# Two graph layers on one core: pauses in rows of gathers, row copies inside layer 1, a first copy on VectorE, x loads on SyncE

## The chip, the cores and the metric

The kernel runs on one core of a Trainium2 chip. The metric is the time of one execution on the device, in microseconds. Three runs of the kernel before took 2118.67, 2122.86 and 2124.68 us; the median, 2122.86 us, is the time that the change is compared with. A change of less than 0.3% of it, about 6.4 us, can hardly be told from no change.

## The reference

There are 4096 nodes with 512 features each, and a symmetric adjacency matrix `adj` of 4096 x 4096, of which some 0.8% is not zero. The two layers are, cut to what matters:

```python
# layer 0
h = relu(layernorm(x))
d = rowsum(adj) ** -0.5
x = x + relu((d[:, None] * adj * d[None, :]) @ h @ W0 + b0)
# layer 1
h = relu(layernorm(x))
e = leaky_relu(h @ W1 @ a_top + (h @ W1 @ a_bottom).T, 0.2)
p = softmax(where(adj > 0, e, -1e12))
n = -softmax(where(adj > 0, -e, -1e12))
x = x + elu(concat([p @ h, n @ h]) @ wtrans)
```

Layer 0 is a dense product with all of `adj`. In layer 1 only the places where `adj` is not zero count, so each row needs just the h rows of its neighbours.

## The kernel before, in words

**Layer 0.** The 4096 rows are 32 tiles of 128 rows, numbered j. The output tiles are made in eight groups, `GROUPS = ((26, 6), (16, 4), (20, 4), (0, 4), (4, 4), (8, 4), (12, 4), (24, 2))`, each given as its first tile and number of tiles. Group 0 is multiplied plainly while the rows of `adj` are summed and x is normalized and projected. The other groups multiply 2 x 2 blocks with seven products in place of eight (`multiply_blocks`, L893, on the sums that `sum_at` makes at L880 to L883). A group of four holds seven of the eight PSUM banks, so the next group's products can begin only as the banks of the last one are read out. `join_blocks` (L764 to L797) does that at the start of the next group: ScalarE copies half a bank (L773), VectorE adds another half to it (L774), and three to five more VectorE instructions follow for every pair of output tiles. Then `finish0` (from L803) makes the result of one tile at a time: it adds x (L806), stores x1 for later, normalizes, makes h, and writes h into the tables (L813 to L824).

**Tables.** Layer 1 gathers rows from eight tables in DRAM, one for each eighth of the output rows. All have the same h rows (516 words) and each has its own mask bytes (128 words). `tab0`, which is 4, is the table that layer 1 reads first. `finish0` writes h to `tab0` by a GpSimd DMA (L814), and to the other seven by `put_row` (L443): for most tiles seven ScalarE DMAs (L821 to L823); for the tiles 12 to 15, that is `GROUPS[-2]`, the 28 puts are collected in `puts` and issued by SyncE at the end of the last group (L1213 to L1214); for the tiles 24 and 25, the last group, SyncE writes table 0 (L819) and ScalarE writes the six others within layer 1, one for each of the first 12 row blocks (L1362 to L1364).

**x.** `load_xr` (L743 to L745) loads the x tile that `finish0` adds. It is a GpSimd DMA. There are two buffers, so the load for the third and fourth tile of a group waits until VectorE has used the first and second one.

**Lists.** VectorE makes, for every pair of row blocks, lists of the rows that it needs (L391, L393), and GpSimd scatters these (L413), one indirect DMA after the other.

**Layer 1.** There are 64 row blocks of 64 rows, in pairs. For a pair 22 chunks of 128 rows are gathered, in three parts a = 0, 1, 2 of 8, 6 and 8 chunks; each chunk is one indirect DMA on GpSimd (L451) of 128 rows of 2576 bytes. The even block of a pair uses the parts 0 and 1, the odd block 1 and 2. VectorE and ScalarE make the weights of a block (`scores` L463, `exps` L469 to L473, `mask_out` L480, `tree` L485 to L491), TensorE multiplies 14 chunks (L1305), ScalarE scales the result (L1314), TensorE turns it (L506) and, once a pair, multiplies by wtrans (L1328). The first pair, `PAIR0`, is gathered and begun within the last group of layer 0: `gather0(1)`, `gather0(2)` and `gather0(0)` are called at the steps 4, 7 and 10 of that group. A verdict on the lists (L1027 to L1030) is then loaded by every engine, which branches to `sparse_layer1`. Its first gathers are the three parts of `pairs[0]`, then of `pairs[1]`. In `gather1` a small GpSimd copy that reads the last chunk of part 2 (L1269 to L1273) keeps GpSimd from going on before that chunk has landed; it is there for the pairs with index k = 1 to 5.

**Order.** The framework's scheduler places instructions on each engine by its own estimate of when they are ready; `keep_in_program_order` ties one behind all that was written for its engine before it. An instruction that waits holds up all that is queued behind it on its engine, DMA issues on SyncE, ScalarE and GpSimd included.

Of the kernel before, what the change touches and what calls it, by code (L numbers as in the profile page):

```python
# [259 lines left out]
def gcn_gat_kernel(  # L260
# [181 lines left out]
    def put_row(queue, g, j, h):  # L442
        return queue.dma_start(  # L443
            out=rows_of(g, j // EJ)[:, j % EJ, :ROW_W], in_=h.bitcast(I32)
        )

    def gather(gt, n, a):

        c = sum(CHUNKS[:a])
        for k in range(CHUNKS[a]):  # L450
            nc.gpsimd.indirect_dma_start(  # L451
                out=gt[:, k, :],
                out_offset=None,
                in_=table[2 * n // RPT],
                in_offset=bass.IndirectOffsetOnAxis(
                    ap=idx[n // NH][:, n % NH, c + k : c + k + 1], axis=0
                ),
            )
# [56 lines left out]
    with sbuf(name="y0", bufs=1) as y_pool, sbuf(name="wa", bufs=1) as wa_pool, sbuf(name="bits", bufs=4) as bits_pool, sbuf(name="small0", bufs=4) as small, ExitStack() as rest, ExitStack() as lists:  # L515
# [226 lines left out]

        def load_xr(j):  # L743
            xrs[j] = xin.tile([P, F], F32, tag="xr", name=f"xr{j}")
            nc.gpsimd.dma_start(out=xrs[j], in_=x[j * P : (j + 1) * P, :])  # L745

        def affine(y, acc, j):

# [16 lines left out]
        def join_blocks(i0, n, acc, work, new_w):  # L765

            ys = {}
            for x in range(n // 2):
                p16, p23, p45, p7 = acc[x]
                j0, j1 = i0 + x, i0 + n // 2 + x  # L770
                ys[j0], ys[j1] = y, v = [new_y(work, j, -1) for j in (j0, j1)]
                w = new_w(f"w{j0}")[:, :H]
                nc.scalar.copy(y[:, :H], p16[:, :H])  # L773
                nc.vector.tensor_tensor(w, p16[:, H:], y[:, :H], ALU.add)  # L774
                nc.vector.tensor_tensor(y[:, H:], p45[:, H:], w, ALU.add)

                def first(p23=p23, y=y):
                    nc.vector.tensor_tensor(y, p23, y, ALU.add)

                def second(p7=p7, w=w, p45=p45, v=v):  # L780
                    two = "p (a f) -> p a f"
                    nc.vector.tensor_tensor(w, p7, w, ALU.add)
                    nc.vector.tensor_tensor(
                        v.rearrange(two, a=2),
                        p45.rearrange(two, a=2),
                        w.unsqueeze(1).to_broadcast([P, 2, H]),
                        ALU.add,
                    )

                if n == 2:  # L790
                    first()
                    affine(y, y, j0)
                    second()
                    affine(v, v, j1)
                else:
                    second()
                    first()  # L797
            if n > 2:
                for j, y in ys.items():
                    affine(y, y, j)  # L800
            return ys

        def finish0(work, j, y, h, prod):  # L803

            xt = xrs.pop(j)
            nc.vector.scalar_tensor_tensor(y, y, 0.0, xt, ALU.max, ALU.add)  # L806
            nc.gpsimd.dma_start(out=x1_dram[j], in_=y)
            nc.gpsimd.memset(h[:, ROW_T + 1 :], 0.0)
            normalize(h[:, :F], y, f"b{j}")

            def dot(g, vec):
                nc.vector.scalar_tensor_tensor(
                    prod(f"prod{j}_{g}"), h[:, :F], 1.0, wa_bc[g], ALU.mult, ALU.mult, accum_out=vec  # L813
                )  # L814

            dot(1, h[:, ROW_T : ROW_T + 1])
            put_row(nc.gpsimd, tab0, j, h)
            if late0 <= j < late0 + n_late:
                put_row(nc.sync, 0, j, h)  # L819
            elif GROUPS[-2][0] <= j < sum(GROUPS[-2]):  # L820
                puts.extend(partial(put_row, nc.sync, g, j, h) for g in others)  # L821
            else:
                for g in others:  # L823
                    put_row(nc.scalar, g, j, h)  # L824
            dot(0, s_all[:, j : j + 1])
            nc.vector.tensor_copy(t_all[:, j : j + 1], h[:, ROW_T : ROW_T + 1])
# [156 lines left out]
                mark()  # L983
        pending = (GROUPS[0], partial(evict, i0, acc))
        listing, joining, spare = [], [], []
        puts = []

        def make_lists(g):
            make_keys(g)
# [130 lines left out]
        with sbuf(name="work2", bufs=2) as work, sbuf(name="sums2", bufs=2) as sum_pool, sbuf(name="at2", bufs=4) as at_pool, sbuf(name="scratch", bufs=1) as scratch, sbuf(name="pair", bufs=1) as pair:  # L1120
# [7 lines left out]
            def gather0(a):  # L1128
                if a < 2:
                    k = 1 - a  # L1130
                    gt = y_pool.tile([P, Y_PARTS[k] * F], F32, tag=f"y{k}", name=f"g0_{a}")
                else:
                    gt = t_pool.tile([P, T_PARTS[0] * 3 * H], F32, tag="t0", name=f"g0_{a}")
                gt = gt[:, : CHUNKS[a] * ROW].bitcast(I32)
                gts[a] = gt.rearrange("p (k c) -> p k c", c=ROW)
                gather(gts[a], PAIR0, a)

            def parts0(r):
                a = r % 2
# [59 lines left out]
            def step(jp):  # L1199
                if jp == 0:  # L1200
                    nc.scalar.dma_start(
                        out=s_pair,
                        in_=s_dram[PAIR0 * P : (PAIR0 + 1) * P].partition_broadcast(P),
                    )
                if jp == 4:
                    gather0(1)
                if jp == 7:
                    gather0(2)
                if jp == 10:
                    gather0(0)  # L1210
                    weights0(blocks[0])
                if jp == NP - 1:
                    for put in puts:  # L1213
                        tc.keep_in_program_order(put())  # L1214
                    weights0(blocks[1])
                    warm = small.tile([P, 1], F32, tag="warm", name="warm2", bufs=1)
                    tc.keep_in_program_order(
                        nc.scalar.activation(warm, ones[:, 0:1], AF.Sqrt)
                    )
# [20 lines left out]
    def sparse_layer1():  # L1240
        with ExitStack() as pools:
# [22 lines left out]
            def gather1(n, a):  # L1264
                k = pairs.index(n)
                gt = g_pools[k % 2, a].tile([P, CHUNKS[a], ROW], I32, tag="g", name=f"g{a}_{n}")
                gather(gt, n, a)
                gath.setdefault(n, []).append(gt)
                if a == 2 and 0 < k < 6:  # L1269

                    mark = small.tile([P, 1], I32, tag="mark", name=f"mark{n}", bufs=1)
                    i = nc.gpsimd.tensor_copy(mark, gt[:, CHUNKS[a] - 1, 0:1])
                    tc.keep_in_program_order(i)  # L1273

            def parts(r):

# [67 lines left out]
            pairs = [(PAIR0 + n) % (NR // 2) for n in range(1, NR // 2)]  # L1344
            order = [r for n in pairs for r in (2 * n, 2 * n + 1)]
            first = order[:4]
            later = [*range(tab0 + 1, NTAB), *range(1, tab0)]
            wanted = list(dict.fromkeys(r // 8 for r in order))
            for _ in range(2):
                tc.keep_in_program_order(load_s(wanted.pop(0)))  # L1350
# [8 lines left out]
            weights(order[1])  # L1359
            for k, r in enumerate(order):  # L1360
                product(r)
                if k < n_late * len(later):  # L1362
                    g, m = later[k // n_late], k % n_late
                    tc.keep_in_program_order(put_row(nc.scalar, g, late0 + m, late_h[:, m]))  # L1364
                if k + 4 - k % 2 < len(order):
                    for a in ((0,), (1, 2))[k % 2]:
                        gather1(order[k + 4 - k % 2] // 2, a)
# [20 lines left out]
        sparse_layer1()  # L1388
    with branch.Else():
        dense_layer1(  # L1390
            tc, adj_t, wtrans, out, x1_dram, table[0], s_all, t_all, ident, ones, load_adj_t, bank
        )


# [28 lines left out]
```

## Time and profile before

| What | Value |
|---|---|
| Median of the timed runs | 2122.86 us |
| The profiled execution's own time | 2154.57 us |
| Its span | 2153.1 us |
| TensorE busy | 2010.9 us, 93% |
| VectorE busy | 1115.9 us, 52% |
| ScalarE busy | 517.8 us, 24% |
| GpSimd busy | 942.3 us, 44% |
| Mean DMA rate | 243 GB/s |
| Mean granted TensorE clock | 0.969 |

A line of the waits view reads: the engine and its line, what released it, total idle time in us, times, longest. A line of the windows view gives for a stretch of time each engine's busy time with its number of instructions, the granted TensorE clock, the mean busy share of the 16 DMA engines and GB/s. A line of the timeline gives start, duration, engine, line, operation, tiles, and in brackets the idle time before and its releaser. "issue" is idle time for which the profile shows no wait, "remote" a release of which it doesn't know the source. PE is TensorE's matmul, PEld its weight load, DVE is VectorE, ACT is ScalarE, POOL is GpSimd and SP is SyncE.

### The profile page before, as it was taken

The page shows a single profiled execution, that of the slowest core. Times are in us where ns is not written, and L with a number is a line of the kernel's source. Part 1 is how long each engine was busy: PE and PEld are TensorE (multiplying, and loading weights), DVE is VectorE, ACT ScalarE, POOL GpSimd, SP SyncE. Part 2 cuts the span into 40 slices and gives each one's busy share as a digit, 9 for nine tenths or more (in the row PEclk, how much of TensorE's full clock was granted, in tenths as well). Part 3 has the DMA queues.
Part 4 walks back from the last instruction along what each step waited for, and adds up shares of the span by engine and source line. Part 5 has one row for each costly group of instructions (what it writes and reads, how often), then busy time and mean ns, then how long its engine had stood idle before and what let it go on. Part 6 is the DMA issues. An engine that isn't in the chain of part 4 may idle for free.

```text
span 2153.1 us, 20102 instructions
## 1 busy us (share of the span) xinstructions
PE 2010.9 (93%) x6456; PEld 1184.8 (55%) x6456; DVE 1115.9 (52%) x2791; ACT 517.8 (24%) x889; POOL 942.3 (44%) x1017
## 2 busy tenths in 40 slices
PE   7998999999998979899639999999999999999998
PEld 3443447888776868787414444444444444444443
DVE  5444536463896469834605645445354455455441
ACT  4645612223331310001102221212122222122120
POOL 2010102121123310323365767777777777777740
PEclk9999999999998989999869999999999999999999
DMA  9988918796977885456787878878788888888850
GB/s 376 367 300 326 366 35 295 256 317 197 338 222 245 259 251 174 150 181 191 271 260 224 267 239 254 253 239 242 235 255 242 251 240 238 254 242 239 246 179 21
DMA packets 186441, 524.12 MB, mean 243 GB/s; under 512 B 25683, under 2 KB 34867, under 8 KB 186326
## 3 DMA queue, kind: packets, MB, share of 16 engines
q0 software_dynamic: 73856, 283.61, 43.2%
q1 hardware_dynamic: 82592, 184.90, 25.2%
q10 hardware_dynamic: 29878, 54.24, 7.1%
q8 instruction: 52, 0.85, 0.2%
q14 instruction: 63, 0.52, 0.1%
HBM read 419.73 MB, written 102.92 MB: 243 GB/s over the span
## 4 chain that ended last, share of the span: by engine, by line
PE 55%; DVE 5%; another core or an unknown queue 3%; issue 1%; ACT 0%; DMA 0%; DVEq 0%; ACTq 0%
PE u L1305 35%; PE o L1328 10%; PE p L893 8%; PE tp L506 1%; DVE keys L393 1%; DVE lst L391 1%; PE cs L496 0%; DVE p L480 0%; DVE sums L880 0%; DVE sums L881 0%; DVE sums L882 0%; DVE sums L883 0%; DMA at<-in_adj_t 0%; DVE y L749 0%
## 5 line engine op out<-in xcount | busy, mean ns | idle before, releaser
L451 POOL DMA_INDIRECT g<-table,idx x704 | 751.0, 1067 | 283.5 <-issue 196.5
L1305 PE MATMUL u<-g,p 128*128 128x512 f32 x1736 | 762.8, 596 | 3.4 <-DVE p L480 3.1
L1305 PEld LDWEIGHTS u<-g,p 128*128 128x128 f32 x1736 | 325.7, 191 | 392.0 <-issue 379.1
L893 PE MATMUL p<-y,at 128*128 128x256 f32 x832 | 255.2, 389 | 18.5 <-DVE w L774 7.1
L893 PE MATMUL p<-t,sums 128*128 128x256 f32 x832 | 251.7, 387 | 14.9 <-DVE sums L881 9.6
L463 DVE TENSOR_TENSOR z<-g,s 128x512 f32<-128x512 f32 (+1 forms) x124 | 77.3, 624 | 353.8 <-DMA g<-table,idx 285.3
L893 PE MATMUL p<-y,sums 128*128 128x256 f32 x832 | 253.4, 387 | 2.4 <-issue 2.4
L1328 PE MATMUL o<-wt_sb,ut 128*128 128x512 f32 x512 | 225.1, 592 | 0.5 <-ACT ut L510 0.5
L473 ACT ACTIVATE p<-z 128x896 f32<-128x896 f32 (+2 forms) x136 | 115.8, 900 | 307.1 <-issue 220.2
L893 PEld LDWEIGHTS p<-y,at 128*128 128x128 f32 x832 | 159.8, 194 | 45.6 <-DVE w L774 8.0
L893 PEld LDWEIGHTS p<-t,sums 128*128 128x128 f32 x832 | 159.9, 194 | 43.0 <-DVE sums L881 13.7
L852 PE MATMUL acc<-y,at 128*128 128x512 f32 x384 | 176.4, 597 | 2.4 <-ACT y L700 2.4
L893 PEld LDWEIGHTS p<-y,sums 128*128 128x128 f32 x832 | 161.8, 195 | 26.0 <-issue 2.8
L480 DVE SCALAR_TENSOR_TENSOR p<-g,p 128x384 f32<-128x384 uint8 (+1 forms) x256 | 143.3, 620 | 56.8 <-ACT p L473 34.2
L725 POOL DMA_DIRECT2D table<-m x71 | 54.2, 765 | 258.1 <-ACT m L714 127.7
L1328 PEld LDWEIGHTS o<-wt_sb,ut 128*128 128x128 f32 x512 | 94.8, 190 | 107.8 <-issue 107.1
L714 ACT ACTIVATE m<-at 128x1024 uint8<-128x1024 f32 (+1 forms) x110 | 105.6, 988 | 193.6 <-DMA at<-in_adj_t 146.8
L893 PE MATMUL p<-t,at 128*128 128x256 f32 x416 | 127.7, 389 | 18.5 <-DVE w L774 17.2
L677 PE MATMUL yp<-w_sb,hx_t 128*128 128x512 f32 x256 | 124.6, 633 | 15.8 <-ACT y L700 13.4
L1314 ACT ACTIVATE us<-u,rl 128x512 f32<-128x512 f32 x62 | 42.6, 687 | 354.2 <-issue 203.4
L880 DVE TENSOR_TENSOR sums<-at 128x256 f32<-128x256 f32 x104 | 43.3, 417 | 149.8 <-PE p L893 87.1
L852 PEld LDWEIGHTS acc<-y,at 128*128 128x128 f32 x384 | 71.2, 192 | 81.5 <-issue 78.4
(183 smaller groups left out, 1746.3 us busy)
## 6 DMA issues: line engine op xcount, KB each, us to landing
at<-in_adj_t SPq DMA_DIRECT2D x136, 512.0 KB
ar<-in_adj SPq DMA_DIRECT2D x128, 512.0 KB
table<-h ACTq DMA_DIRECT2D x182, 258.0 KB
table<-m POOLq DMA_DIRECT2D x55, 256.0 KB
at<-in_adj_t SPq DMA_DIRECT2D x32, 384.0 KB
g<-table,idx POOLq DMA_INDIRECT x704
xr<-in_x POOLq DMA_DIRECT2D x32, 256.0 KB
x<-x1d SPq DMA_DIRECT2D x32, 256.0 KB
```

The source lines that it names most:

```text
L451: nc.gpsimd.indirect_dma_start(out=gt[:, k, :], out_offset=None, in_=table[2 * n // RPT], in_offset=bass.IndirectOffsetOnAxis(ap=idx[n // ...
L463: return nc.vector.tensor_tensor(z, t.to_broadcast([P, n, RB]), s.unsqueeze(1).to_broadcast([P, n, RB]), ALU.add)
L473: nc.scalar.activation(p[:, :, g, :], z, AF.Exp, scale=(1.0, -1.0)[g])
L480: nc.vector.scalar_tensor_tensor(e, m, 0.0, e, ALU.is_gt, ALU.mult)
L677: nc.tensor.matmul(yp, hx_t[j][:, c * P : (c + 1) * P], w0_sb[:, c, :], start=c == 0, stop=c == FC - 1,)
L714: nc.scalar.activation(m, at, AF.Sign)
L725: nc.gpsimd.dma_start(out=rows_of(t, e)[:, c:, ROW_W + (a - t * TT) * P // 4 : ROW_W + (b - t * TT) * P // 4], in_=masks[i0][:, c:, (a - i ...
L852: nc.tensor.matmul(a, at[:, 0, it * P : (it + 1) * P], y0[j], start=j == 0, stop=j == NJ - 1)
L880: op(t[:, 0], a[:, :, 0, 1], a[:, :, 1, 1], ALU.add)
L893: i = nc.tensor.matmul(out, left[:, x * P : (x + 1) * P], right, start=jp == 0 and first, stop=jp == NP - 1 and (final or not first),)
L1305: nc.tensor.matmul(u, p[:, k0 + k].rearrange("p g c -> p (g c)"), gt[:, k, :F].bitcast(F32), start=k0 + k == 0, stop=k0 + k == nk - 1,)
L1328: nc.tensor.matmul(po, ut[:, g, c, :], wt_sb[:, g * FC + c, :], start=g == 0 and c == 0, stop=g == 1 and c == FC - 1,)
```

## The change

Four edits. A helper `pause` holds the small GpSimd copy, and it is called at three more places: after `gather0(2)` in the last group of layer 0, after part 1 of `pairs[0]` and after part 0 of `pairs[1]`. The h rows of the tiles 12 to 15 and 24 to 25 are no longer put into the other tables from SBUF; within layer 1, at the row blocks k = 1, 7, 13, 19, 25, 31 and 37, SyncE issues two DMAs that copy these 768 rows from `tab0` to one other table, from DRAM to DRAM. The first copy of `join_blocks` goes from ScalarE to VectorE, and `load_xr` from GpSimd's queue to SyncE's. The other branch, which doesn't run here, reads `tab0` in place of table 0.

```diff
+    def pause(pool, gt):
+        mark = pool.tile([P, 1], I32, tag="mark", name="mark", bufs=1)
+        i = nc.gpsimd.tensor_copy(mark, gt[:, gt.shape[1] - 1, 0:1])
+        tc.keep_in_program_order(i)
...
         def load_xr(j):
             xrs[j] = xin.tile([P, F], F32, tag="xr", name=f"xr{j}")
-            nc.gpsimd.dma_start(out=xrs[j], in_=x[j * P : (j + 1) * P, :])
+            nc.sync.dma_start(out=xrs[j], in_=x[j * P : (j + 1) * P, :])
...
-                nc.scalar.copy(y[:, :H], p16[:, :H])
+                nc.vector.tensor_copy(y[:, :H], p16[:, :H])
...
             put_row(nc.gpsimd, tab0, j, h)
-            if late0 <= j < late0 + n_late:
-                put_row(nc.sync, 0, j, h)
-            elif GROUPS[-2][0] <= j < sum(GROUPS[-2]):
-                puts.extend(partial(put_row, nc.sync, g, j, h) for g in others)
-            else:
+            if all(not j0 <= j < j0 + n for j0, n in GROUPS[-2:]):
                 for g in others:
                     put_row(nc.scalar, g, j, h)
...
                 gather(gts[a], PAIR0, a)
+                if a == 2:
+                    pause(small, gts[a])
...
                 if jp == NP - 1:
-                    for put in puts:
-                        tc.keep_in_program_order(put())
                     weights0(blocks[1])
...
-                if a == 2 and 0 < k < 6:
-                    mark = small.tile([P, 1], I32, tag="mark", name=f"mark{n}", bufs=1)
-                    i = nc.gpsimd.tensor_copy(mark, gt[:, CHUNKS[a] - 1, 0:1])
-                    tc.keep_in_program_order(i)
+                if (k, a) in ((0, 1), (1, 0)) or a == 2 and 0 < k < 6:
+                    pause(small, gt)
...
-            later = [*range(tab0 + 1, NTAB), *range(1, tab0)]
+            later = [*range(tab0 + 1, NTAB), *range(tab0)]
+            def copy_rows(g, j, n):
+                r = j // EJ * ER + j % EJ * P
+                return nc.sync.dma_start(
+                    out=table[g][r : r + n * P, :ROW_W], in_=table[tab0][r : r + n * P, :ROW_W]
+                )
...
-                if k < n_late * len(later):
-                    g, m = later[k // n_late], k % n_late
-                    tc.keep_in_program_order(put_row(nc.scalar, g, late0 + m, late_h[:, m]))
+                if k % 6 == 1 and k // 6 < len(later):
+                    for j, n in GROUPS[-2:]:
+                        tc.keep_in_program_order(copy_rows(later[k // 6], j, n))
```

More of the change, by code (lines that the diff above doesn't have):

```diff
@@ L985, in gcn_gat_kernel @@
         listing, joining, spare = [], [], []
-        puts = []
         def make_lists(g):
@@ L1390, in gcn_gat_kernel @@
         dense_layer1(
-            tc, adj_t, wtrans, out, x1_dram, table[0], s_all, t_all, ident, ones, load_adj_t, bank
+            tc, adj_t, wtrans, out, x1_dram, table[tab0], s_all, t_all, ident, ones, load_adj_t, bank
         )
```

## The prediction

> **What bounds the kernel now.** I read the page first, then the windows, the waits of TensorE, and the timeline where it stands still. TensorE is the bound nearly everywhere, so only its idle time is for sale.
>
> ```profile
> span 2153.1 us, 20102 instructions
> PE 2010.9 (93%) x6456; PEld 1184.8 (55%) x6456; DVE 1115.9 (52%) x2791; ACT 517.8 (24%) x889; POOL 942.3 (44%) x1017
> ```
>
> That leaves 142 us. Some 30 us of it lie in group 0, which the change doesn't touch. For the rest, the windows (the gathers in layer 0's last group; the start of the layer 1 gathers; the stretch after it; layer 1's steady part):
>
> ```profile
> 1008.00:1040.00 32.00, 21.45 (x92) 16.91 (x91) 6.46 (x15) 1.54 (x2) 21.15 (x22) 0.90 0.96 344
> 1070.35:1088.00 17.65, 17.65 (x39) 7.39 (x38) 2.28 (x9) 0.76 (x3) 13.46 (x14) 0.88 0.78 229
> 1088.00:1131.50 43.50, 5.46 (x19) 2.88 (x17) 0.65 (x4) 2.02 (x4) 28.46 (x30) 0.58 0.82 253
> 1300.00:2060.00 760.00, 759.70 (x1979) 350.85 (x1978) 373.39 (x692) 158.51 (x261) 562.06 (x519) 1.00 0.82 244
> ```
>
> The steady part has no idle TensorE: nothing is to be gained there, only lost. From 1088 to 1131.5 us TensorE, VectorE and ScalarE all do next to nothing while GpSimd issues gather upon gather. Who waits for whom there, on TensorE, and in layer 0 from 300 us on:
>
> ```profile
> PE tp L506 <- ACT us L1196: 25.3, 1, 25.3
> PE tp L506 <- issue: 12.8, 1, 12.8
> PE ok_ps L1027 <- DVE all_ok L1024: 7.3, 1, 7.3
> ...
> PE p L893 <- DVE w L774: 24.3, 5, 7.8
> PE p L893 <- issue: 10.4, 5, 4.1
> PE p L893 <- DVE sums L881: 9.6, 5, 4.3
> PE p L893 <- ACT y L773: 6.8, 1, 6.8
> ```
>
> The timeline shows that no real work is behind the 38 us at L506:
>
> ```profile
> 1090.01 0.28 PE L496 MATMUL cs<-ones,total 128*128 128x1 f32 x2
> 1103.67 0.17 DVE L498 RECIPROCAL rl<-cs 128x1 f32<-128x1 f32 x1 [30.50 <-remote]
> 1105.77 0.43 PE L496 MATMUL cs<-ones,total 128*128 128x1 f32 x2
> 1124.43 0.95 POOL L451 DMA_INDIRECT g<-table,idx  x1 [0.30 <-issue]
> 1125.37 0.65 ACT L510 COPY ut<-tp 128x256 f32<-128x256 f32 x2 [20.57 <-remote]
> 1130.35 0.17 DVE L498 RECIPROCAL rl<-cs 128x1 f32<-128x1 f32 x1 [26.31 <-remote]
> 1135.73 14.05 PE L1305 MATMUL u<-g,p 128*128 128x512 f32 x28 [3.13 <-DVE p L480]
> ```
>
> TensorE's sum is issued at 1090.01, VectorE uses it 13.7 us later; the next one is used 24.6 us later. All is let go within 5 us of the last of 44 gathers, which GpSimd issued from 1070.35 on without a break, one each 1.25 us. The 22 gathers from 1008.49 show the same in small (10.4 us "issue"). I read it so: what engines need to go on gets through slowly while a row of gathers has no break. In the steady part GpSimd is nearly as busy but often waits for buffers.
>
> **What the Trainium skill says.** "TensorE: Matmul & The Clock Gate", Part 1: after an idle window of about 3.4 us TensorE falls to half clock. The trace agrees: after 6.75 us idle at 760 us a pair of matmuls takes 1.2 us, otherwise 0.59, and the last gap window has clock 0.58. So a gap costs more than its length. "DMA: Bandwidth & Descriptors", Queues, rings and completion order: DMA engines go round among queues packet by packet; the trace can't show the order, but gathers and 28 puts together reach 397 GB/s (1025 to 1050 us), gathers alone 284. Same page, Anatomy of one DMA: some 2 us from issue to completion; here GpSimd's existing pause waited twice, 6.6 us in all, so 3.3 us each, and that value I use. "Runtime: NRT & Kernel Launch", Instruction fetch mechanics: instructions come by DMA in 16 KiB blocks, and a branch can force a fetch. The page has 52 packets, 0.85 MB in all, on an instruction queue, 16 KB each; whether a fetch is what is late here, no view tells.
>
> **The change, part by part, against the span of 2153.1 us.**
>
> *Pause and puts in layer 0's last group.* Removed: 28 SP puts of 258 KB (7.4 MB, 35 us in flight from 1013.68) and two more. The wait at issue is 10.4 us, with half clock after it some 13 us. But behind it the third part's gathers are next: 22 x 1.253 from 1008.49 is 1036, with the pause 3.3 and landing 3.3 us 1042.7, and VectorE uses them at 1047.2. So only **4.5 us** get through, 0 to 10 as bounds (all of it if the join is placed ahead of these weights; nothing if the pause releases nothing).
>
> *Pauses in layer 1's start.* From the first gather (T) to TensorE's first layer 1 matmul there are 1135.7 - 1070.35 = 65.4 us. Without the stall: block 32's product and the late rows end at T + 21.8 (1092.1), the second block's sum, scale and turn take 3, load and branch 1.3, the first weights 4 us (1131.75 to 1135.73): T + 29 or so. The stall is thus **36 us**. With a pause after 14 gathers, 14 x 1.253 = 17.5 us, the row breaks just where the stall began (1088). What is late next is supply: pair 1's part 1 is issued by T + 36 x 1.253 + 2 x 3.3 = T + 52, landed T + 55, weights T + 59, while two blocks of 12.3 us from T + 29 end at T + 54: 5 us idle. wtrans (2 MB), s, x1 and the first copy (1.6 MB read, 1.6 written) now lie beside the gathers rather than after them, as wtrans does at 1131.45: 2 us more, 0 to 5. Net **29 us** in the profiled execution. The scheduler may put a gather or two ahead of the pause, as it did with the old ones (two gathers stand before the one at 1147.58); then the break is under 1 us and may not be enough.
>
> *How much of that is in timed runs.* The profiled execution took 2154.57 us, 31.7 more than the median. If all of that is the stall made longer by profiling, 46.8 - 31.7 = 15 us of 36 + 10.4 are real, 0.32; if none, all. I take 0.6. The 7 us of supply stay: 0.6 x (36 + 4.5) - 7 = **17 us**, between 0.32 x 40.5 - 7 = 6 and 33.
>
> *First copy on VectorE.* 13 copies of 0.35 to 0.37 us on ScalarE become as many on VectorE; its add of the same shape takes 0.42, so I take 0.42. What goes is ScalarE's queue: it sits behind masks that wait for adjacency tiles. At 541 us TensorE waited 3.8 us and at 655 3.3 us for the second copy, with VectorE idle 3.7 and 4.3: both go, 7 us and some 2 for the clock. Against that, where VectorE is late itself, the copy lies on the path: at 767 ScalarE's copy let four matmuls run before VectorE came at 773.6 (up to 2 us lost), at 884 two copies (0.8), at 980 and in the last join 0.4 each. Net **5 us**, -1 to 9.
>
> *x by SyncE.* At 680 us VectorE waited 13.4 us for x behind GpSimd's list scatters, and again 3.4; TensorE then idled 3.8 and 0.7 us and ran at half clock for 3.4 us. That goes: **4 us**, 6 at most. On SyncE the load waits for its buffer (VectorE L806) with the adjacency loads queued behind; SyncE has run up to six tiles ahead by then and itself waits 228 us for TensorE, so I cost it at nothing; if it isn't covered, see the last rival.
>
> *Copies in layer 1.* Gone: 12 ScalarE puts (3.1 MB). Added: 14 SP DMAs, seven bursts of 768 rows, 11.1 MB read and written. At 240 to 400 GB/s for read plus written bytes a burst is 8 to 13 us of traffic, once in three pairs of 32.4 us. A pair's 22 gathers take 27.6 us, so 4.8 us a pair is spare, 14 in three. In the steady part masks are ready some 25 us before their product. At the start there is no such lead: I take **3 us**, 0 to 8. The x1 loads and stores behind them on SP have slack of the same kind.
>
> **Sum:** 17 + 5 + 4 - 3 = 23, so 2122.86 - 23 is about **2099.5 us** (profiled: 4.5 + 29 + 9 - 3 = 40 off 2153, some 2113).
>
> **Rivals.**
> *The stall stays* (0.20): the break is too short, or something else, such as a fetch at the branch, holds the engines. For it: the old pauses let two gathers by. Against: release came 5 us after the row's end. Then joins and x give 9, fewer puts 2, copies cost 3: 8 us, 2115.
> *Nothing is left in timed runs* (0.12): the stall is the profiler's, joins and x give 9, copies cost 3, late supply 5: about 2122. Against: 31.7 us isn't 46.8.
> *x blocks SyncE* (0.13), slower: at six group starts two x loads wait for the first and second L806, 5 and 10 us after the join begins (437.3 and 442.6 after 432.4); adjacency tiles behind them come after that plus some 4 us, while TensorE needs one each 6 us and holds two: 2 to 8 us lost a group. From 4 us a group, 24 in all, it outweighs the gain of 23; at 6 us, 36 in all, 2135. Against: the scheduler orders SP by readiness, so tiles whose buffers are free go first.
>
> **How the numbers follow.** Forecast 0.55 at 2099.5, own range 2073 (all real, 33 + 9 + 6) to 2114. Low end 2073; the high end 2124 takes in the first two rivals and leaves the last out. 0.3% is 6.4 us, about what a measurement can tell from no change. Faster: 0.53 of the forecast, 0.15 of the first rival, 0.02 of the second: 0.70. Same: 0.17. Slower: 0.13.
>
> **What would show it.** Right: TensorE's waits at L506 fall from 38 us to under 8; the first L1305 matmul comes some 30 us after the first layer 1 gather; the L893 "issue" wait is gone; L774's waits fall from 24 to about 15; no VectorE wait for xr above 3 us; in the steady part TensorE stays full. Wrong: VectorE's L498 still waits over 10 us there, or new TensorE waits at L1305 on masks over 15 us, or adjacency tiles late at group starts.

## The result, and the profile after

The changed kernel takes 2121.56 us (median of 20 runs, 2116.69 to 2128.36) against 2123.44 us for the kernel before (20 runs beside it). The ratio is 0.9988 with an interval of 0.9977 to 0.9999: 2.5 us less, 0.2 to 4.9, no change that counts. The forecast was 2099.5.

Its profiled execution took 2128.36 us; it is the slowest of those 20 runs. The page's first lines and the four windows that answer to those of before, moved with the work (gathers in layer 0's last group; the start of the layer 1 gathers; the stretch after it; the steady part):

```profile
span 2126.5 us, 20058 instructions
PE 2008.1 (94%) x6456; PEld 1184.0 (56%) x6456; DVE 1121.1 (53%) x2804; ACT 511.4 (24%) x876; POOL 915.8 (43%) x988
```

```profile
1006.00:1038.00 32.00, 31.98 (x145) 26.88 (x144) 13.42 (x28) 3.33 (x4) 22.19 (x23) 1.00 0.85 259
1062.30:1080.00 17.70, 17.70 (x39) 7.41 (x38) 2.50 (x10) 0.76 (x3) 13.43 (x15) 0.90 0.78 231
1080.00:1123.50 43.50, 38.19 (x98) 17.72 (x97) 22.15 (x45) 11.50 (x25) 29.73 (x31) 0.92 0.93 325
1300.00:2060.00 760.00, 760.00 (x1981) 351.49 (x1980) 374.92 (x692) 155.13 (x261) 553.55 (x524) 1.00 0.84 257
```

In the third line TensorE works 38.19 of 43.50 us, where it was 5.46. The waits of TensorE from 300 to 1200 us say the same; the 38 us of the transposes (L506, now L512) are down to 1.2:

```profile
PE p L895 <- DVE w L780: 17.3, 3, 7.8
PE ok_ps L1028 <- DVE all_ok L1025: 15.7, 1, 15.7
PE p L895 <- DVE sums L883: 13.1, 3, 9.0
...
PE u L1303 <- DVE p L486: 4.1, 1, 4.1
PE cs L502 <- DVE total L497: 3.5, 1, 3.5
...
PE tp L512 <- ACT us L1199: 1.2, 1, 1.2
```

The timeline behind the first pair shows each sum (`cs`) and each set of transposes (`tp`) read by VectorE or ScalarE within 0.7 us:

```profile
1081.73 0.28 PE L502 MATMUL cs<-ones,total 128*128 128x1 f32 x2
...
1082.04 0.17 DVE L504 RECIPROCAL rl<-cs 128x1 f32<-128x1 f32 x1 [16.66 <-PE cs L502]
...
1083.67 0.60 PE L512 MATMUL tp<-ident,us 128*128 128x128 f32 x4
...
1084.11 0.28 PE L502 MATMUL cs<-ones,total 128*128 128x1 f32 x2
1084.31 0.65 ACT L516 COPY ut<-tp 128x256 f32<-128x256 f32 x2 [1.13 <-PE tp L512]
1084.49 0.17 DVE L504 RECIPROCAL rl<-cs 128x1 f32<-128x1 f32 x1 [2.09 <-PE cs L502]
...
1090.35 15.29 PE L1303 MATMUL u<-g,p 128*128 128x512 f32 x28 [4.06 <-DVE p L486]
```

So nearly every sign that the prediction asked for is there (only VectorE's longest wait for x, 3.4 us, is above the 3 us that it allowed): the first layer 1 product comes 28.0 us after the first gather (65.4 before), the "issue" wait at L893 is gone, L774's wait went from 24.3 to 17.3 us. The spans of the two profiled executions differ by 26.6 us (2153.1 and 2126.5), the timed runs by 2.5. That gap is what the experiments are about.

Two things follow from the traces alone. First, the first layer 1 product is 45.4 us earlier (1090.3 for 1135.7), but from there to the last product layer 1 takes 1028.5 us in place of 1009.1: 19.4 us come back, where the prediction had 7 for supply and 3 for copies. Most of this is supply, and it reaches TensorE through the order of work on VectorE: VectorE makes the weights of a later block before it reads the sum of the present one, and where it first has to wait for a gather, TensorE waits too. Here it waits 5.7 us for a gather, and reads the sum of 1240.68 only 13.8 us after it was issued:

```profile
1240.68 0.38 PE L502 MATMUL cs<-ones,total 128*128 128x1 f32 x2 [0.58 <-DVE total L497]
...
1246.36 0.56 DVE L469 TENSOR_TENSOR z<-g,s 128x384 f32<-128x384 f32 x1 [5.73 <-DMA g<-table,idx]
...
1254.46 0.16 DVE L504 RECIPROCAL rl<-cs 128x1 f32<-128x1 f32 x1
...
1256.47 0.76 PE L512 MATMUL tp<-ident,us 128*128 128x128 f32 x4 [3.28 <-ACT us L1312]
```

The same comes again at 1295 us. From block 9 to block 12 of layer 1 the lead over the kernel before falls from 37.8 to 24.8 us.

Second, two theories of the gap could be named before any experiment: the profiler itself stretched the standstill (theory 1), or the standstill is real and its gain is given back later in layer 1 (theory 2).

### The profile page after: what moved, and what is told of

Same layout as the page of the kernel before. It is cut to its first block, busy times and chain, and to the rows that moved or that the text cites. A ratio compares the mean times of both kernels' runs of the same rounds, so it can differ in the third digit from the quotient of the medians.

```text
span 2126.5 us, 20058 instructions
## 1 busy us (share of the span) xinstructions
PE 2008.1 (94%) x6456; PEld 1184.0 (56%) x6456; DVE 1121.1 (53%) x2804; ACT 511.4 (24%) x876; POOL 915.8 (43%) x988
## 4 chain that ended last, share of the span: by engine, by line
PE 47%; DVE 7%; DMA 5%; POOL 5%; issue 3%; ACT 1%; ACTq 0%; DVEq 0%; SPq 0%; POOLq 0%
PE u L1303 31%; PE o L1326 9%; PE p L895 5%; POOL g L457 5%; DMA g<-table,idx 2%; DMA at<-in_adj_t 2%; DVE keys L393 1%; DVE lst L391 1%; PE tp L512 1%; DMA table<-h 1%; ACT m L720 1%; DVE p L486 0%; DVE prod L818 0%; PE cs L502 0%; ACTq L443 0%
## 5 line engine op out<-in xcount | busy, mean ns | idle before, releaser
L457 POOL DMA_INDIRECT g<-table,idx x704 | 742.6, 1055 | 261.6 <-issue 191.6
L895 PE MATMUL p<-t,sums 128*128 128x256 f32 x832 | 249.4, 385 | 13.1 <-DVE sums L883 13.1
L895 PEld LDWEIGHTS p<-y,sums 128*128 128x128 f32 x832 | 161.0, 194 | 30.1 <-DVE sums L885 7.4
L895 PE MATMUL p<-t,at 128*128 128x256 f32 x416 | 126.6, 387 | 18.9 <-DVE w L780 17.3
L413 POOL DMA_INDIRECT ld<-li,off x48 | 43.9, 915 | 158.3 <-DMA ld<-li,off 108.1
```

The lines of the kernel that those rows point to most:

```text
L413: return nc.gpsimd.indirect_dma_start(out=lst_dram[g][:, :], out_offset=bass.IndirectOffsetOnAxis(ap=off[g][:, e, c : c + 1], axis=0), in_ ...
L457: nc.gpsimd.indirect_dma_start(out=gt[:, k, :], out_offset=None, in_=table[2 * n // RPT], in_offset=bass.IndirectOffsetOnAxis(ap=idx[n // ...
L895: i = nc.tensor.matmul(out, left[:, x * P : (x + 1) * P], right, start=jp == 0 and first, stop=jp == NP - 1 and (final or not first),)
```

## The experiments

The runs fell on four chips; on which one the comparison above ran is not on record. On each of them the kernel before took 2148 to 2152 us (medians of 19 to 62 runs), never 2123. Ratios below are to the kernel before on the same chip.

**Cut after four blocks.** Both kernels, with layer 1 ended after its first four row blocks.

```diff
+            order = order[:4]
             for _ in range(2):
                 tc.keep_in_program_order(load_s(wanted.pop(0)))
```

> The kernel before, with layer 1 ended after its first four row blocks (the output rows of all other blocks are left out), so that the time ends right behind the start of the layer 1 gathers. To be compared with the same cut of the changed kernel. Theory 1 (the standstill in the row of gathers is there only in the profiled execution): its profiled execution is 25 to 40 us longer than its timed median, and its timed median is within 6 us of the other cut's. Theory 2 (the standstill is in every run, and what the pauses gain is given back later in layer 1): profiled and timed agree within 6 us, and its timed median is 35 to 45 us above the other cut's.

> The changed kernel with the same cut after four row blocks of layer 1 (all other output rows are left out). Both theories: its profile is about 40 us shorter than that of the other cut, and profiled and timed times of this one differ by under 10 us. Theory 1: timed, it is 0 to 6 us shorter than the other cut. Theory 2: timed, it is 35 to 45 us shorter.

Measured: 1193.78 us (5 runs, 1187.44 to 1198.66, the profiled one 1187.44) for the kernel before, 1192.57 us (6 runs, 1181.56 to 1198.99, the profiled one 1193.23) for the changed one. The execution whose profile is kept is not longer than the others, which speaks against theory 1. Theory 2's 35 to 45 us are not there either, but the cuts can't decide on it, because both cut kernels stand still. That of the changed one does so before its first product, which comes 51.4 us after the first gather. In the cut kernel before the first eight gathers are 1.53 to 1.60 us apart in place of 1.25, what TensorE passes on is read at once at first, and the first product comes after 31.1 us. Then its second product stands still: the matmuls come one by one, and VectorE reads the sum of 1105.63 only 18.5 us later:

```profile
1080.06 0.60 PE L506 MATMUL tp<-ident,us 128*128 128x128 f32 x4
...
1080.69 0.65 ACT L510 COPY ut<-tp 128x256 f32<-128x256 f32 x2 [1.13 <-issue]
...
1105.63 0.28 PE L496 MATMUL cs<-ones,total 128*128 128x1 f32 x2
...
1114.01 1.32 PE L1305 MATMUL u<-g,p 128*128 128x512 f32 x2 [1.51 <-issue]
...
1117.54 1.01 PE L1305 MATMUL u<-g,p 128*128 128x512 f32 x1 [2.21 <-issue]
...
1124.10 0.17 DVE L498 RECIPROCAL rl<-cs 128x1 f32<-128x1 f32 x1 [21.29 <-PE u L1305]
```

**The pauses alone, and all but the pauses.** The first is the kernel before with `pause` and its three new calls; the second is the changed kernel with

```diff
-                if a == 2:
-                    pause(small, gts[a])
...
-                if (k, a) in ((0, 1), (1, 0)) or a == 2 and 0 < k < 6:
+                if a == 2 and 0 < k < 6:
```

> The kernel before with the three new pauses alone. Theory 1: timed 2118 to 2124 us (0 to 5 us gained), profiled 25 to 40 us below the profiled kernel before, so some 2115 to 2130. Theory 2: the pauses gain some 30 us in timed runs and the copies, the join and x give it back, so this kernel is at 2090 to 2100 timed.

> The changed kernel without its three new pauses. Theory 1: timed 2118 to 2124, as the changed kernel; profiled 25 to 40 us more than timed, since the standstill is back in the profile. Theory 2: timed 2145 to 2160, since the other edits alone cost some 30 us.

Measured: the pauses alone 2147.10 us, ratio 0.9981 (0.9966 to 0.9995), 4.1 us less; all but the pauses 2152.78, ratio 1.0004 (0.9993 to 1.0015). Neither theory foretold this. Profiled and timed times agree (2150.40 and 2156.73 profiled), so the 31.7 us between the profiled execution and the median, on which the prediction built, are not what the profiled execution adds to the others of its occasion. And the pauses end only a part of the standstill here: the first product comes 47.0 us after the first gather, against 67.4 without them.

**The two kernels themselves, on one chip.** No edit. From here on theory 3: the standstill is not the same everywhere, and where it is missing the pauses have nothing to remove.

> The kernel before, unchanged, profiled and timed on one chip, because the first runs showed that profiled and timed times agree within 0.3% and that the kernel before takes 2152 us on one occasion and 2123 us on another. Theory 1, as first put (the profiler makes the standstill): dead if profiled and timed agree here with the standstill in the trace. Theory 3 (the standstill at the start of layer 1 is on some chips or occasions and not on others, and where it is missing the pauses have nothing to remove): if the median here is near 2152, the trace shows TensorE's transposes at L506 waiting 35 us or more; if it is near 2122, they wait under 10 us.

> The changed kernel, unchanged, beside the kernel before. Theory 2 (pauses remove a real standstill of 36 us and layer 1 gives it back): its first layer 1 product comes under 32 us after its first layer 1 gather everywhere, and the time is 0 to 5 us below the kernel before. Theory 3: where the kernel before takes 2152 us the pauses break the standstill only in part, so the first product comes 40 to 60 us after the first gather, and the time is 2140 to 2152; where it takes 2122 it comes some 28 us after it, and the time is 2118 to 2124.

Measured: the kernel before 2147.29 us (profiled 2144.93); the changed kernel 2142.13, ratio 0.9970 (0.9957 to 0.9984), 6.4 us less. On another chip the changed kernel, run again, took 2141.29, ratio 0.9949 (0.9929 to 0.9970), 11.0 us less:

> The changed kernel beside its variant without the old pauses. From the earlier run: 4 to 9 us below the kernel before where that takes 2150 us, within 4 us of it where it takes 2122.

The timeline of the kernel before, behind the first pair:

```profile
1090.53 0.66 PE L506 MATMUL tp<-ident,us 128*128 128x128 f32 x4 [2.17 <-issue]
...
1091.02 0.28 PE L496 MATMUL cs<-ones,total 128*128 128x1 f32 x2
...
1106.17 0.65 ACT L510 COPY ut<-tp 128x256 f32<-128x256 f32 x2 [15.70 <-remote]
...
1111.86 0.17 DVE L498 RECIPROCAL rl<-cs 128x1 f32<-128x1 f32 x1 [22.15 <-remote]
```

and of the changed kernel on the same chip:

```profile
1086.46 0.66 PE L512 MATMUL tp<-ident,us 128*128 128x128 f32 x4 [1.61 <-issue]
...
1086.95 0.28 PE L502 MATMUL cs<-ones,total 128*128 128x1 f32 x2
...
1095.11 0.65 ACT L516 COPY ut<-tp 128x256 f32<-128x256 f32 x2 [8.71 <-remote]
...
1099.38 0.17 DVE L504 RECIPROCAL rl<-cs 128x1 f32<-128x1 f32 x1 [13.75 <-remote]
...
1112.44 14.63 PE L1303 MATMUL u<-g,p 128*128 128x512 f32 x28 [10.81 <-DVE p L486]
```

The same code, the same row with the same pause (here at 1084.4), and transposes that ScalarE copied 0.6 us after their start in the comparison's profile are copied after 8.7 us here. That is the first half of theory 3, shown. The first product comes 48.4 us after the first gather, against 59.3: 10.9 us of the 36 that I gave the pauses. The other half of theory 3, that the kernel before has no standstill where it takes 2123 us, was to be seen in two more executions of it:

> The kernel before, one look, to catch it where it takes 2122 us. There, theory 3 says that TensorE's waits at L506 behind the first pair are under 10 us and the first layer 1 product comes 28 to 45 us after the first gather. Where it takes 2150: 55 to 66 us, as seen twice.

> The kernel before, one look, once more to catch it where it takes 2122 us. There: lags from TensorE's transposes and sums behind the first pair to their readers under 3 us, and the first layer 1 product 28 to 45 us after the first gather. Where it takes 2150: lags of 10 to 25 us, 55 to 66 us.

Both took some 2150 (2146.13 and 2143.47 us; 57.1 and 60.0 us to the first product). So it stays unseen.

**A rival that no run tests: the recording.** Every timed run on record has a span and a granted clock of its own, so something was recorded in all of them, and that profiled and timed times agree doesn't clear the recording itself. The kept traces give reason to ask. They hold all instructions (20058 in both traces compared here), but where the kernel before takes 2150 us they lack records of landed transfers. The changed kernel's trace from the comparison has 25053 such records, its trace beside the kernel before has 17529. Up to 1060 us the two hold nearly the same, 12730 and 12366; after it, where layer 1's gathers begin, 12323 and 5163. All other traces, the first one of the kernel before among them, lack them too. Their pages therefore show no time to landing for the gathers; here the line of the comparison's page, then of the other:

```profile
g<-table,idx POOLq DMA_INDIRECT x704, 4.2
```

```profile
g<-table,idx POOLq DMA_INDIRECT x704
```

So the engines stand still in the traces in which the profiler loses records. Whether recording holds the engines up there, or one cause does both, stays open. Loss alone is not enough: the cut kernel before loses as many around 1080 us, where its handovers are quick.

**GpSimd held until the others are through.** This ends the standstill in another way than a pause does.

```diff
-            for a in range(3):
+            for a in range(2):
                 gather1(pairs[0], a)
+            weights(order[0])
+            hold(order[0])
+            gather1(pairs[0], 2)
...
+            weights(order[1])
+            hold(order[1])
             for a in range(3):
                 gather1(pairs[1], a)
-            weights(order[0])
-            weights(order[1])
```

`hold(r)` is a GpSimd copy of one word out of the last chunk of block r's weights.

> The kernel before, with GpSimd held twice at the start of layer 1: after 14 gathers until the first block's weights are there, and after 8 more until the second block's weights are there. So the other engines pass work on while no row of gathers runs. Theory 3: where the kernel before takes 2152 us the standstill goes, the first layer 1 product comes 27 to 36 us after the first gather in place of 65, some 10 us of later supply come back, and the time falls by 12 to 25 us; where it takes 2122 it gains nothing, 0 to 8 us slower. Rival (what is late is not the row of gathers but the branch or an instruction fetch): the first product still comes 55 us or more after the first gather, and the time does not fall.

Measured: the first product comes 32.4 us after the first gather, as expected, and the time is 2151.07, ratio 1.0015 (1.0001 to 1.0030). Nothing of the gain is left in the time. The window from 1150 to 1200 us, of the held kernel and then of the kernel before, shows where it went:

```profile
1150.00:1200.00 50.00, 34.68 (x82) 15.36 (x80) 21.47 (x38) 7.90 (x12) 37.06 (x38) 0.85 0.86 276
```

```profile
1150.00:1200.00 50.00, 50.00 (x133) 23.27 (x132) 29.27 (x55) 11.31 (x20) 35.22 (x35) 1.00 0.87 266
```

TensorE is idle for 15.3 us while GpSimd is as busy as before. By the trace block 0 starts 26.5 us before that of the kernel before (1100.9 for 1127.5), block 4 still 18.7, block 5 only 3.2. Block 5's masks had been ready for 24.5 us when it began, and TensorE's four transposes before it started 1.4 to 2.8 us apart, where they otherwise take 0.6 us together: not supply, but the same standstill in a later row.

**A gap behind every gather.** The kernel before, for the first two pairs:

```diff
+            if gap:
+                t = gap.tile([P, 256], F32, tag="gap", name="gap", bufs=1)
+                tc.keep_in_program_order(nc.gpsimd.memset(t, 0.0))
```

> The kernel before with a small GpSimd fill of 128 x 256 words behind each of the 44 gathers of the first two pairs. It waits for nothing, so the transfers stay queued as before, but GpSimd's issues have gaps. If it is the issuing of gathers that holds back what the other engines pass on, more gets through in the gaps: from TensorE's transposes and sums behind the first pair to their readers 15 and 21 us become under 8, and the first layer 1 product comes 35 to 50 us after the first gather in place of 55 to 60. If it is the queued transfers, or something else, the lags stay at 12 us or more, and the time is 0 to 10 us longer than that of the kernel before.

Measured: gathers come 1.45 us apart in place of 1.25, and everything gets through at once:

```profile
1088.04 0.60 PE L509 MATMUL tp<-ident,us 128*128 128x128 f32 x4
...
1088.48 0.28 PE L499 MATMUL cs<-ones,total 128*128 128x1 f32 x2
1088.68 0.65 ACT L513 COPY ut<-tp 128x256 f32<-128x256 f32 x2 [1.13 <-PE tp L509]
...
1088.86 0.17 DVE L501 RECIPROCAL rl<-cs 128x1 f32<-128x1 f32 x1 [2.09 <-PE cs L499]
...
1095.47 14.54 PE L1308 MATMUL u<-g,p 128*128 128x512 f32 x28 [4.81 <-DVE p L483]
```

The first product comes 27.8 us after the first gather, better than I had expected, and the time is 2146.93, ratio 0.9986 (0.9969 to 1.0003). Against the kernel before on that chip, block 0 starts 30.6 us earlier, block 6 15.2, block 14 0.2. The first loss is supply: the first 44 gathers took 67.8 us in place of 54.0, and block 2's masks were ready 8.5 us after its product had begun. The second loss, in the blocks 11 to 14, has masks ready 13 to 25 us ahead; there the gathers have no gaps any more. Some 5 of its 15 us are again TensorE behind VectorE, which makes a later block's weights first. In the other 10, around the start of block 13, TensorE's instructions come 1 to 3 us apart and wait for nothing that the trace shows: the standstill again. The lost records fit this run too: from 1080 to 1140 us, while the gaps last, it has 637 landings on record, against 110 in the kernel before on that chip.

**The old pauses taken away.** The changed kernel with

```diff
-                if (k, a) in ((0, 1), (1, 0)) or a == 2 and 0 < k < 6:
+                if (k, a) in ((0, 1), (1, 0)):
```

> The changed kernel with its three new pauses but without the five old ones (pairs 1 to 5). If the start of layer 1 is bound by GpSimd's supply once TensorE starts earlier, each pause taken away gives back up to 3.3 us of it and the first pairs gain 5 to 15 us. If it is the row of gathers that holds the engines up whenever their lead is small, the longer rows bring new waits with no cause in the blocks 4 to 12, and the time is 5 to 30 us longer.

> The changed kernel without the five old pauses, once more, now beside the changed kernel. If the supply at the start of layer 1 is what takes the gain of the three new pauses, it is 2 to 8 us faster than the changed kernel, and its TensorE has masks ready 25 us ahead from block 10 on where the changed kernel has some 20 to 25 only later. If the first result was chance: within 2 us.

Measured: ratios 0.9958 (0.9934 to 0.9981) and 0.9952 (0.9935 to 0.9970), 9.0 and 10.3 us less than the kernel before; beside the changed kernel's 0.9970 and 0.9949 on the same chips that is 3 us better once and equal once, so the two are not told apart. The feared new waits in the blocks 4 to 12 did not come (in the second run the lead over the kernel before is 8.7 us at block 4 and at block 14). The changed kernel, five old pauses in place, had one there in the slowest of its six executions. With block 12's masks ready 13.1 us before, its product took 26.2 us in place of 12.1, matmul by matmul (TensorE's rows of the timeline alone):

```profile
1315.67 1.71 PE L1303 MATMUL u<-g,p 128*128 128x512 f32 x2 [1.40 <-issue]
1318.47 1.01 PE L1303 MATMUL u<-g,p 128*128 128x512 f32 x1 [1.08 <-issue]
1319.89 1.01 PE L1303 MATMUL u<-g,p 128*128 128x512 f32 x1 [0.41 <-issue]
1321.29 1.87 PE L1303 MATMUL u<-g,p 128*128 128x512 f32 x2 [0.39 <-issue]
```

**Small gaps in all of layer 1.** The changed kernel with a fill of 128 x 1 or 128 x 128 words behind each layer 1 gather, and no pauses in layer 1.

> The changed kernel with a GpSimd fill of 128 x 1 words behind each gather of layer 1, and none of the pauses there, new or old (the pause in layer 0's last group stays). If any GpSimd instruction between two gathers lets the other engines go on, there is no unexplained wait of TensorE in layer 1, gathers still come each 1.25 to 1.35 us, the lead is kept and the time is 15 to 28 us below that of the kernel before where that takes 2150. If the gap must have a length (0.33 us of fill gave a cadence of 1.45), the lags of 10 to 20 us are back and the time is 0 to 10 us from the kernel before, on either side.

> The same with a fill of 128 x 128 words, half of that in the spread run, behind each gather of layer 1. Cadence by interpolation 1.31 to 1.38 us, so 29 to 30 us a pair against TensorE's 32.4: supply keeps up, some 5 us are lost in the first pairs. If half the gap is enough: lags under 1 us behind the first pair, no later standstill in the blocks 4 to 14, 15 to 25 us below the kernel before where that takes 2150. If not: within 8 us of it.

Measured: 2138.69, ratio 0.9948 (0.9933 to 0.9963), and 2139.57, ratio 0.9950 (0.9930 to 0.9970): 11.2 and 10.7 us less than the kernel before, the changed kernel's own gain within the intervals. The small fill fits into the pause that gathers have anyway (they still come each 1.25 us) and passes take up to 15.5 us. With the larger one (1.34 us apart) the first product comes 33.4 us after the first gather, but 15 of its 18 us of lead over the small fill are gone by block 3: VectorE read the sum of 1106.09 us only after 11.5 us, with the same gaps still in place.

**The other parts.** Joins and x without the rest; the row copies without the rest; the changed kernel without the row copies.

```diff
-                nc.scalar.copy(y[:, :H], p16[:, :H])
+                nc.vector.tensor_copy(y[:, :H], p16[:, :H])
...
-            nc.gpsimd.dma_start(out=xrs[j], in_=x[j * P : (j + 1) * P, :])
+            nc.sync.dma_start(out=xrs[j], in_=x[j * P : (j + 1) * P, :])
```

> The kernel before with the first copy on VectorE and x by SyncE, nothing else. My forecast: 9 us faster (5 for the joins, 4 for x), -1 to 15; the rival of x blocking SyncE: 10 us or more slower, with TensorE waiting for adjacency tiles at the starts of groups 2 to 6. From the run without pauses, whose layer 0 ended 7 us earlier with copies and puts changed too: 5 to 8 us faster.

> The kernel before with the row copies alone (no SyncE puts in layer 0's last group, no ScalarE puts in layer 1, seven bursts of copies from table to table). My forecast: 3 us slower in layer 1, 0 to 8. The run without the pauses spent 7.5 us more in layer 1 than the kernel before and won some 7 in layer 0, so if the copies carry that, this kernel is 4 to 9 us slower than the kernel before; if the copies are hidden, it is within 3 us.

> The changed kernel with the old puts in place of the row copies, that is the kernel before with pauses, join and x. If the copies cost what their run alone showed against the kernel before (7.7 us, 3 to 12), this kernel is 5 to 12 us faster than the changed one, some 10 to 15 us faster than the kernel before where that takes 2150, and is the best of all. If that cost was chance, as the trace of that run says (no block of its layer 1 was later than in the kernel before), it is within 3 us of the changed kernel.

Measured: joins and x 2146.01, ratio 0.9986 (0.9973 to 0.9998), 3.0 us less; the copies alone 2155.40, ratio 1.0036 (1.0016 to 1.0057), 7.7 us more; without the copies 2144.52, ratio 0.9988 (0.9972 to 1.0004), so not better than with them. The last two contradict each other. In the trace of the copies alone no block of layer 1 starts more than 0.4 us later than in the kernel before, but this trace is of the fastest of its nine executions (2145.06 us). What the copies cost is not settled: the interval of their run alone reaches from 3 to 12 us, past the 8 us of the prediction's bounds.

## Why the prediction was wrong

**The step that failed** is "How much of that is in timed runs". It took the 31.7 us between the profiled execution and the median for a stretch that profiling may add, put 0.6 on what is left, and so counted 17 us; the whole change measured 2.5. The cut kernels and the two kernels on one chip show that a profiled execution takes what timed ones of its occasion take (2144.93 and a median of 2147.29). What lies between is something that I had not on my list: the kernel before takes 2123 us in the comparison and some 2150 in every other run. The profiled 2154.57 us fits the second: its sums are read after 13.7 and 24.6 us, and in each of the three later traces of the kernel before the second block's sum is read after 20 to 22 us. I had worked from the trace of one and reckoned against the median of the other. Likewise the 26.6 us between the two profiled executions are no measure of the change: on one chip the profiled spans differ by 6.8 (2143.5 and 2136.7).

Three sums of the prediction are slightly off. 36 + 10.4 is 46.4, not 46.8; the terms of T + 29 add to 30.1; and 33 + 9 + 6 below the median is 2075, not 2073. None of them moves the forecast by more than a microsecond.

**The rival "nothing is left in timed runs"** had the right time, 2122, with the wrong reason. The likelier reason is that the standstill is missing, or nearly so, wherever the kernel takes 2123 us. For it: in the comparison's profile of the changed kernel, handovers take 0.3 to 0.7 us, while the same kernel takes 8 us and more elsewhere. And both kernels are faster in the comparison, the one before by some 25 us and the changed one by 20, so the difference lies in the occasion and not in the change. As no trace of the kernel before from there exists, this is argued and not shown, and what makes the occasions differ, the recording perhaps, is not known. If layer 0's 8 us hold there too, layer 1 must lose some 5 us against the kernel before (8 less 2.5), by its three more stops of GpSimd, the copies or the late gathers shown above.

**"The row breaks just where the stall began"**: it does, and the engines go on, but some 3 us later the next row holds them again. Where the standstill exists the pauses won 10.9 us (59.3 to 48.4) and 11.8 us (60.0 to 48.2), not 36.

**"What is late next is supply", 5 + 2 us**: the right kind, and too small. After the standstill was ended altogether, 30.6 us of lead were gone by block 14: some 15 to supply, some 5 to VectorE's order of work, and some 10 to the standstill's return in a later row. The last two no line of my sum had. That is the reading I would change most: the standstill gives GpSimd time to get 44 gathers ahead, and this lead covers all that comes later. Without it TensorE runs close behind the gathers, and every row that holds it up costs time.

**Joins and x**, 9 us in the profile: right in kind, and about twice too large. From the first to the last product of the groups 1 to 6 the first two profiles differ by 7.9 us, and on one chip the kernel before takes 647.1 us, the changed kernel 639.4 and joins and x alone 641.2. But these are good cases: over all kept traces the nine with the old joins take 644.6 us in the mean (640.7 to 647.1), the eleven with the new ones 640.2 (637.6 to 641.8), 4.4 less. Timed, 3.0 us of joins and x are seen. The rival of x blocking SyncE is out: TensorE waited only once for an adjacency tile from 300 us to layer 1's start, 2.6 us in the changed kernel and 4.4 in joins and x alone. VectorE's longest wait for x fell from 13.4 us to 3.4:

```profile
DVE spare L812 <- DMA xr<-in_x: 5.1, 3, 3.4
```

**The pause in layer 0's last group**, 4.5 us: from the end of group 6 to the verdict it is 84.9 and 79.7 us in the first two profiles (5.2 less), but 83.8 and 84.9 on one chip, so what the pause gains there was seen in one trace only. In it TensorE finishes earlier and then waits for the verdict (7.3 us before, 15.7 after).

**A late instruction fetch**, which the prediction left open, is not what the records show: between 1088 and 1131.5 us the profiled kernel before moved packets on two queues only, neither of them an instruction queue. Nor was anything fetched during the slow product of block 12 above, from 1311 us: the instruction queues of that trace moved nothing from 1293 to 1345 us.

```profile
q0 software_dynamic: 2544, 10.47, 76.9%
q1 hardware_dynamic: 288, 0.52, 4.7%
```

## What to carry to other kernels

Before a profile's stall is priced against a median, see that both come from the same chip or at least from executions of the same length: here 31.7 us between them was the warning, and one run of the unchanged kernel with a profile would have told. A stall that lets another engine get ahead is also that engine's lead; removing it pays only as far as the work behind it can be supplied without that lead, so follow the start of each later block, not just the first. Where the same wait ends early and comes back two blocks later with its inputs ready, the cause was not removed but moved. And see whether the trace is whole before its "issue" and "remote" are read: a page without times to landing has lost records, here just where the engines stood still.

## What the runs showed of the hardware

How soon TensorE's results reached their readers at the start of layer 1 went with the gaps between GpSimd's gathers, where the kernel before takes 2150 us. The table has the first pair's sums of the second block, from their start to VectorE's reciprocal, and its first and second transposes, to ScalarE's copy. The fills of 0.12 and 0.22 us were in the changed kernel, that of 0.33 us in the kernel before:

| Behind each gather | Gathers apart, us | Sums to reciprocal, us | Transposes to copy, us |
|---|---|---|---|
| nothing (kernel before) | 1.25 | 20.8 | 15.6 and 11.4 |
| fill of 0.12 us | 1.25 | 15.5 | 10.9 and 8.8 |
| fill of 0.22 us | 1.34 | 1.6 | 0.6 and 5.2 |
| fill of 0.33 us | 1.45 | 0.4 | 0.6 and 0.7 |

It gets worse with the length of the row: in the kernel before, sums issued 18 us into it took 3.1 us, those 23 us into it 20.8. It is not the handover alone: TensorE's matmuls of one product came 1 to 3 us apart with all inputs there. A long queue of unfinished transfers is hardly behind it: the pause waited just 0.89 us for the last of its 14 gathers (the pauses alone), while sums were 3.6 us late. Whether the issuing itself, the lower rate of transfers or the fewer records lets things through is not told apart, since a gap changes all three. Why sums took 0.3 us with the same row in the comparison, and why the kernel before takes 2150 us on four chips and 2123 there, stays open.

None of the variants was faster than the changed kernel beyond its interval; the best ratios, 0.9948 and 0.9949, are the small fill's and the changed kernel's own.
